# Attention values in four column groups of 32, with denominators from sums of two steps

## The chip, the cores and the metric

The kernel runs on one core of a Trainium2 chip. The metric is the device time of one execution in microseconds (us), the median of several runs. The engines are TensorE (PE, with its weight loads PEld), VectorE (DVE), ScalarE (ACT), GpSimd (POOL) and SyncE (SP, which issues the DMAs here).

## The reference

One "macaron" layer over 2048 tokens of width 512: half a feed-forward block, attention, half a feed-forward block, each on a layer-normalised input and added to the residual. Only attention matters here:

```python
x = x + 0.5 * ffn(layernorm(x))
x = x + attn(layernorm(x))
x = x + 0.5 * ffn(layernorm(x))

# attn: 16 heads of 32 columns, 2048 tokens, causal
q, k, v = heads(x @ w_qkv.T + b_qkv)
scores = q @ k.T / sqrt(32) + causal        # causal: -inf above the diagonal
out = softmax(scores) @ v                   # 16 x 2048 x 32
return merge(out) @ w_out.T + b_out
```

All is in 32-bit floats.

## The kernel before

**Tiling.** The 16 heads are worked in eight head pairs, p = 0 to 7. For a pair the queries go in four blocks of 512 (g = 0 to 3), the keys in chunks of 128 (c). A block g meets the chunks 0 to 4g + 3: the first 4g lie wholly below the diagonal (a *whole step*), the last four cross it (a *diagonal step*; the four of a block are called a quad here). In a diagonal step the first `off` = 0, 128, 256 or 384 queries of the block are left out. So a head pair has 4 + 8 + 12 + 16 = 40 steps. In block 3 six whole steps come first, then the quad, then six whole steps (`around`); in the other blocks the quad comes last.

**One step** (`attend`, `step`). For both heads of the pair (index a) TensorE writes the scores, transposed, keys on the partitions, into a PSUM tile `ps`: first a bf16 matmul that puts minus the row maximum there (`maxrows`, L1311), then the 32-row score matmul (L1320). ACT takes exp into `pt`, 128 x 2 x 512 in SBUF (L1343). In a diagonal step the 128 x 128 block on the diagonal is first copied by ACT (L1336), masked by POOL (`affine_select`, L1337), then exponentiated by ACT in place (L1345). Two steps later (`pending`) `values` multiplies `pt` with the values: this is L1250. Its stationary operand is 64 columns wide: 32 columns of a head's values and 32 columns of ones, side by side in `vaug`, so that one matmul gives the output and the softmax denominator of a head. Head 0 writes partitions 0 to 63 of `av`, head 1 partitions 64 to 127; the ones stand in the middle of `vaug` and serve both. `av` is one PSUM bank (`ps_acc`, one buffer).

**After a block** ACT copies `av` to `both` (L1259). The two denominator rows go by DMA to DRAM (`flat`), come back as 16 x 64 (`packs`), DVE takes the reciprocal (L1277) four steps later, and DMAs bring them back (`back`) and spread them to 32 partitions each (`den`, L1282). From eight steps after the copy on, POOL multiplies a quarter of the block per step, one instruction per head (`chunk`, L1289), into `attnT`. For the last head pair (`direct`) the denominators go by one DMA per head to the partitions of the values (L1266), and DVE takes reciprocals of 128 x 128 (L1286).

**Beside it.** While pair p attends, the row maxima of pair p + 1 are made (`maxima`): score matmuls `pm` (L1185) on TensorE, a mask add on the diagonal (L1199) and a maximum (L1200) on DVE, in as many steps, in the same order, so that the diagonal steps of both fall together. The minus maxima are split into three bf16 parts by POOL (L1211, L1214), transposed by TensorE (L1224) and copied by ACT (L1225). All `ps`, `pm` and projection tiles share seven PSUM buffers (`ps_one`). Pairs 0, 2 and 4 carry projections of queries, keys and values for later pairs, pairs 3, 5 and 7 the output projection (`project_out`, L1135), as filling work after their diagonal steps; pairs 1 and 6 carry none. The last pair has no maxima beside it and takes two steps at a time.

**Order.** The program is scheduled by hand: each engine and each queue runs its instructions in the order in which the code issues them. Per step this is: the score matmuls of both kinds; DVE's maxima; ACT's exp; then the values of two steps before; then what falls due in `after_step`.

Of the kernel before, what the change touches and what calls it, by code (L numbers as in the profile page):

```python
# [10 lines left out]
F32 = mybir.dt.float32  # L11
# [5 lines left out]
ALU = mybir.AluOpType  # L17
AX = mybir.AxisListType

P = 128  # L20
# [3 lines left out]
HD = 32  # L24
NT = S // P
# [10 lines left out]
def macaron_kernel(ctx: ExitStack, tc: tile.TileContext, x, packed, scales, wqk, bqk, wv, bv, wo, bo, out):  # L36
# [1004 lines left out]
    def attention(xT, xT_f, wqk_wv, next_w):  # L1041
        with tc.tile_pool(name="aw", bufs=1) as aw, tc.tile_pool(name="qk", bufs=1) as qkp, tc.tile_pool(
            name="pp", bufs=3
# [30 lines left out]
            dens = [qkp.tile([P, 512], F32, tag=f"den{i}", name=f"den{i}") for i in range(2)]  # L1074
            for t in dens:
                nc.gpsimd.memset(t, 1.0)

            vaug = qkp.tile([P, NT, NPAIR // 2, 3 * HD], F32, tag="vaug", name="vaug")
            for t in range(NT):
                nc.gpsimd.memset(vaug[:, t, :, HD : 2 * HD], 1.0)  # L1080
# [24 lines left out]
            def project_v(half):  # L1105


                def piece(t2):
# [11 lines left out]
                    for i in range(2):  # L1120
                        nc.vector.tensor_tensor(
                            vaug[:, 2 * t2 + i, :, :].rearrange("p h (b d) -> p h b d", d=HD)[:, :, ::2, :],
                            ps[:, i, :].rearrange("p (h b d) -> p h b d", b=2, d=HD),
                            bv_sb[:, bass.ts(half, 256)].rearrange("p (h b d) -> p h b d", b=2, d=HD),
                            ALU.add,
                        )
# [107 lines left out]
            def attend(p, width):  # L1234
# [10 lines left out]
                def values(g, c, off, pt):  # L1245
                    if c == 0:
                        avs[0] = ps_acc.tile([P, 512], F32, tag="acc", name=f"av_{p}_{g}")
                    av = avs[0]
                    for a in range(2):
                        nc.tensor.matmul(  # L1250
                            av[64 * a : 64 * a + 64, off:],
                            lhsT=vaug[:, c, p % 4, HD * a : HD * a + 2 * HD],
                            rhs=pt[:, a, off:],
                            start=(c == 0),
                            stop=(c == order(g)[-1]),
                        )
                    if c == order(g)[-1]:
                        both = an.tile([P, 512], F32, tag="both", name=f"both_{p}_{g}")
                        nc.scalar.copy(both, av)  # L1259
                        rc = dens[g % 2]  # L1260
                        direct = p == NPAIR - 1
                        if direct:

                            for a in range(2):
                                v0, d0 = (0, HD) if a == 0 else (3 * HD, 2 * HD)
                                nc.sync.dma_start(out=rc[v0 : v0 + HD, :], in_=both[d0 : d0 + HD, :])  # L1266
                        else:

                            flat = store.tile([2, 512], F32, tag=f"flat{g % 2}", name=f"flat_{p}_{g}")
                            packs = an.tile([16, 64], F32, tag="packs", name=f"packs_{p}_{g}")  # L1270
                            for a in range(2):
                                d0 = HD + HD * a
                                nc.sync.dma_start(out=flat[a : a + 1, :], in_=both[d0 : d0 + 1, :])
                            nc.sync.dma_start(out=packs, in_=flat.rearrange("a (j n) -> (a j) n", j=8))

                        def inverse():
                            nc.vector.reciprocal(packs, packs)  # L1277
                            back = store.tile([2, 512], F32, tag=f"back{g % 2}", name=f"back_{p}_{g}")
                            nc.sync.dma_start(out=back.rearrange("a (j n) -> (a j) n", j=8), in_=packs)
                            for a in range(2):  # L1280
                                v0 = 3 * HD * a
                                nc.sync.dma_start(out=rc[v0 : v0 + HD, :], in_=back[a].partition_broadcast(HD))  # L1282

                        def chunk(j):
                            if direct:
                                nc.vector.reciprocal(rc[:, bass.ts(j, P)], rc[:, bass.ts(j, P)])  # L1286
                            for a in range(2):
                                v = slice(3 * HD * a, 3 * HD * a + HD)
                                nc.gpsimd.tensor_tensor(  # L1289
                                    dst[quadrant(p, a), bass.ts(4 * g + j, P)],  # L1290
                                    both[v, bass.ts(j, P)], rc[v, bass.ts(j, P)], ALU.mult,
                                )
# [3 lines left out]
                        for j in range(4):  # L1296
                            at((3 if direct else 8) + j, lambda j=j: chunk(j))

                def step(g, c, copied):
# [27 lines left out]
                    def rest():  # L1327
# [18 lines left out]
                        pending.append(lambda args=(g, c, off, pt): values(*args))  # L1346
# [5 lines left out]
                for g in range(NB):  # L1352
                    cs = order(g)
                    for n in range(0, len(cs), width):
                        yield [step(g, c, i > 0) for i, c in enumerate(cs[n : n + width])]
# [234 lines left out]
```

## Time and profile before

| | |
|---|---|
| median of 3 runs | 3216.76 us (3214.57 to 3217.85) |
| profiled execution, time | 3218.9 us |
| its span, first to last instruction | 3217.1 us |
| attention within it | about 1294 to 2104 us |
| busy in 1292 to 2104.3 (812.3 us): PE, DVE, ACT, POOL | 803.0, 487.9, 404.4, 218.0 us |
| mean granted TensorE clock | 0.994 |

The profile's page has these parts: busy time of each engine; the span in slices; DMA queues; the chain of work that ended last, followed back from the last instruction; the costliest groups of instructions by line, with busy time, mean duration in ns and the idle time before them; DMA issues. A timeline lists the instructions of one engine in order: start, duration, engine, line, operation, output and inputs, shape, count, and in brackets the idle time before it with its releaser. A 32-bit matmul appears as two MATMUL records, so "x4" at L1250 is one matmul for each head. Records of matmuls that run side by side overlap, and busy sums count them all; the distance from start to start is the safer reading.

### The profile page before, as it was taken

The numbers are of one execution on the slowest core, as the hardware profiler recorded it, in microseconds if no ns is written. First come the engines' busy times: TensorE is split into PE (matmuls) and PEld (weight loads), VectorE is DVE, ScalarE is ACT, GpSimd is POOL, SyncE is SP. The second block draws the span as 40 slices with busy tenths as digits, with TensorE's granted clock in tenths as the row PEclk, the third lists the DMA queues.
The fourth block names the chain that finished last, engine by engine and source line by source line (L and its number), as shares of the span: only waits on it lengthen the run. The fifth ranks groups of instructions, "written<-read, shape, count | busy, mean of one in ns | idle before, by whom it ended". The sixth has DMA issues, their size and how long they took to land.

```text
span 3217.1 us, 39429 instructions
## 1 busy us (share of the span) xinstructions
PE 3168.7 (98%) x14000; PEld 1978.9 (62%) x14000; DVE 2073.8 (64%) x3011; ACT 1059.2 (33%) x2166; POOL 1300.8 (40%) x1404
## 2 busy tenths in 40 slices
PE   7999999999999999999999999999999999999999
PEld 3556565655656575333334333368888878888887
DVE  7676666666566655566564576487666767766675
ACT  5111111111111131455443456533333343333332
POOL 3757585766767560422121123213222232223222
PEclk9999999999999999999999999999999999999999
DMA  3222221212222200000000000054344445344441
GB/s 137 87 83 109 89 92 62 95 66 89 90 82 107 105 33 7 5 15 7 13 6 6 28 20 8 7 179 140 114 130 131 121 132 164 116 127 128 124 125 59
DMA packets 258851, 260.36 MB, mean 81 GB/s; under 512 B 20392, under 2 KB 221096, under 8 KB 254688
## 3 DMA queue, kind: packets, MB, share of 16 engines
q1 hardware_dynamic: 258656, 257.85, 24.7%
q8 instruction: 111, 1.82, 0.2%
q14 instruction: 84, 0.69, 0.1%
HBM read 176.28 MB, written 79.92 MB: 80 GB/s over the span
## 4 chain that ended last, share of the span: by engine, by line
PE 93%; DVE 2%; ACT 2%; issue 1%; POOL 1%; DMA 0%; SPq 0%; POOLq 0%; DVEq 0%; ACTq 0%
PE d_f L737 12%; PE po L438 12%; PE pu L339 12%; PE pg L339 11%; PE av L1250 8%; PE pod_f L866 7%; PE f_f L737 6%; PE pm L1185 6%; PE pqk L1096 4%; PE pof_f L866 3%; PE e_f L737 3%; PE ps L1311 2%; PE pv L1113 2%; PE poe_f L866 2%; PE pp L1135 2%; PE ps L1320 2%
## 5 line engine op out<-in xcount | busy, mean ns | idle before, releaser
L1200 DVE TENSOR_REDUCE parts<-pm 128x1 f32<-128x512 f32 (+3 forms) x640 | 370.6, 608 | 149.6 <-PE pm L1185 134.1
L1185 PE MATMUL pm<-kT,qT 32*128 32x512 f32 (+3 forms) x1280 | 333.9, 574 | 0.1
L737 PE MATMUL d_f<-ys_f,ring 128*128 128x256 f32 x1216 | 321.4, 385 | 7.1 <-DVE o_f L770 7.0
L1343 ACT ACTIVATE pt<-ps 128x512 f32<-128x512 f32 (+3 forms) x576 | 271.7, 532 | 132.0 <-PE ps L1320 131.3
L1250 PE MATMUL av<-pt,vaug 128*64 128x512 f32 (+3 forms) x1280 | 302.1, 556 | 3.4 <-ACT both L1259 2.6
L1320 PE MATMUL ps<-qT,kT 32*128 32x512 f32 (+3 forms) x1280 | 277.9, 533 | 0.0
L737 PEld LDWEIGHTS d_f<-ys_f,ring 128*128 128x128 f32 x1216 | 228.3, 191 | 54.7 <-DVE o_f L770 21.7
L438 PEld LDWEIGHTS po<-wd,inter 128*128 128x128 f32 x1024 | 194.4, 190 | 77.5 <-issue 56.0
L438 PE MATMUL po<-wd,inter 128*128 128x256 f32 x1024 | 241.1, 379 | 0.0
L791 DVE TENSOR_TENSOR o_f<-o_f,o_f 128x1024 f32<-128x1024 f32 x128 | 203.6, 1601 | 57.5 <-ACT o_f L776 53.7
L339 PE MATMUL pg<-xT_f,w 128*128 128x512 f32 x512 | 240.1, 597 | 0.2 <-ACT u L378 0.2
L339 PE MATMUL pu<-xT_f,w 128*128 128x512 f32 x512 | 238.0, 592 | 0.0
L1337 POOL TENSOR_SCALAR_AFFINE_SELECT pt<-pt 128x256 f32<-128x256 f32 x128 | 52.3, 408 | 396.6 <-ACT pt L1336 388.2
L452 POOL TENSOR_TENSOR xq<-xq,d 128x512 f32<-128x512 f32 x124 | 161.6, 1314 | 92.2 <-DVE xq L446 55.9
L1250 PEld LDWEIGHTS av<-pt,vaug 128*64 128x64 f32 x1280 | 65.5, 135 | 205.0 <-issue 147.1
L791 POOL TENSOR_TENSOR o_f<-o_f,o_f 128x1024 f32<-128x1024 f32 x48 | 128.7, 2682 | 142.7 <-ACT o_f L776 141.5
L881 POOL TENSOR_TENSOR xq<-xq,d_f 128x512 f32<-128x512 f32 x48 | 64.8, 1350 | 293.5 <-DVE xq L875 228.1
L438 PE MATMUL po<-wd,s 128*128 128x256 f32 x768 | 181.4, 379 | 0.0
L438 PEld LDWEIGHTS po<-wd,s 128*128 128x128 f32 x768 | 145.5, 190 | 57.9 <-issue 39.9
L339 PE MATMUL pg<-xsum,w 128*128 128x512 f32 x384 | 177.8, 592 | 0.0
L339 PE MATMUL pu<-xsum,w 128*128 128x512 f32 x384 | 177.7, 592 | 0.0
L881 POOL TENSOR_TENSOR xq_second<-xq_second,d_f 128x512 f32<-128x512 f32 x45 | 61.5, 1366 | 272.9 <-DVE xq_second L875 217.6
(214 smaller groups left out, 6090.9 us busy)
## 6 DMA issues: line engine op xcount, KB each, us to landing
wd_f<-kept SPq DMA_DIRECT2D x112, 256.0 KB
kept<-wd SPq DMA_DIRECT2D x8, 1792.0 KB
xq<-in_x SPq DMA_DIRECT2D x16, 256.0 KB
pk<-in_gate_codes SPq DMA_DIRECT2D x16, 256.0 KB
sc<-in_gate_scales SPq DMA_DIRECT2D x32, 128.0 KB
pk<-in_up_codes SPq DMA_DIRECT2D x16, 256.0 KB
sc<-in_up_scales SPq DMA_DIRECT2D x32, 128.0 KB
pk<-in_down_codes SPq DMA_DIRECT2D x16, 256.0 KB
```

The source lines that it names most:

```text
L339: nc.tensor.matmul(ps, lhsT=a[:, j, :], rhs=b[:, j, :], start=(j == 0), stop=(j == 1))
L438: nc.tensor.matmul(ps[:, j, :], lhsT=a[i][:, k, bass.ts(2 * q + j, P)], rhs=b[i][:, k, :], start=(k == 0), stop=(k == 1),)
L452: adder.tensor_tensor(dst, dst, other, ALU.add)
L737: nc.tensor.matmul(ps[:, k, :], lhsT=fa[k][y], rhs=fb[k][y], start=first and k == 0, stop=True, skip_group_check=True,)
L791: sums.append(lambda: eng.tensor_tensor(dst, dst, other, ALU.add))
L866: nc.tensor.matmul(ps[:, j, :], lhsT=a[:, k, bass.ts(2 * q + j, P)], rhs=wd[:, PLACE[i], k, :], start=new and j == k == 0, stop=True, skip ...
L1096: nc.tensor.matmul(ps, lhsT=w[:, j, k, :], rhs=xT[tb][:, k, :], start=(k == 0), stop=(k == 3))
L1185: nc.tensor.matmul(ps[a][:, :n], lhsT=q[r, bass.ts(4 * g + i, P)], rhs=k[r, kb * 512 : kb * 512 + n], start=True, stop=not on_pe,)
L1200: nc.vector.tensor_reduce(parts[:, a, i, kb : kb + 1], ps[a][:, :n], AX.X, ALU.max)
L1250: nc.tensor.matmul(av[64 * a : 64 * a + 64, off:], lhsT=vaug[:, c, p % 4, HD * a : HD * a + 2 * HD], rhs=pt[:, a, off:], start=(c == 0), s ...
L1320: nc.tensor.matmul(ps[a][:, off:], lhsT=k[r, bass.ts(c, P)], rhs=q[r, g * 512 + off : (g + 1) * 512], start=False, stop=True,)
L1343: nc.scalar.activation(pt[:, a, plain:], ps[a][:, plain:], AF.Exp, scale=scale)
```

## The change

The values operand `vals` no longer holds ones: 32 columns per head. The block's queries are taken as two interleaved halves, h = 0 for the 128-query chunks 0 and 2, h = 1 for the chunks 1 and 3. `columns` issues four matmuls of 32 output columns, one for each head and half, each into its own 32 partitions of `av` (partition group 2a + h) and 256 columns wide; `av` is now 128 x 2 x 256, product 0 the values and product 1 the denominators. The denominators come from separate matmuls with a stationary operand of ones (`ones_f`), once per two steps: the `pt` of two successive steps are added first, and the sum is multiplied. The addition runs on POOL, one instruction per head, for pairs of steps that start at offset 0 both; on DVE, one instruction for both heads with a copy of the columns that only one of the steps has, for the diagonal pairs, and for all pairs of steps of the last head pair. The last two steps of a head pair are not added, and get two sets of denominator matmuls. A sum made in step n is used by the matmuls of step n + 3 (n + 2 at a block's end). `pt` gets four buffers for three, the sums two. Values and denominators of a query now lie on the same partitions, so the last pair needs no DMA for them, and its reciprocals take two chunks at once; the other pairs send four rows of 256 out and back for two of 512.

```diff
-            name="pp", bufs=3
+            name="pp", bufs=4
...
-            dens = [qkp.tile([P, 512], F32, tag=f"den{i}", name=f"den{i}") for i in range(2)]
-            for t in dens:
-                nc.gpsimd.memset(t, 1.0)
-
-            vaug = qkp.tile([P, NT, NPAIR // 2, 3 * HD], F32, tag="vaug", name="vaug")
-            for t in range(NT):
-                nc.gpsimd.memset(vaug[:, t, :, HD : 2 * HD], 1.0)
+            dens = [qkp.tile([P, 256], F32, tag=f"den{i}", name=f"den{i}") for i in range(2)]
+
+            vals = qkp.tile([P, NT, NPAIR // 2, 2 * HD], F32, tag="vals", name="vals")
+            ones_f = aw.tile([P, HD], F32, tag="ones_f", name="ones_f")
+            nc.gpsimd.memset(ones_f, 1.0)
...
-                            vaug[:, 2 * t2 + i, :, :].rearrange("p h (b d) -> p h b d", d=HD)[:, :, ::2, :],
-                            ps[:, i, :].rearrange("p (h b d) -> p h b d", b=2, d=HD),
-                            bv_sb[:, bass.ts(half, 256)].rearrange("p (h b d) -> p h b d", b=2, d=HD),
-                            ALU.add,
+                            vals[:, 2 * t2 + i, :, :].rearrange("p h d -> p (h d)"), ps[:, i, :],
+                            bv_sb[:, bass.ts(half, 256)], ALU.add,
...
-                def values(g, c, off, pt):
-                    if c == 0:
-                        avs[0] = ps_acc.tile([P, 512], F32, tag="acc", name=f"av_{p}_{g}")
-                    av = avs[0]
+                def columns(product, operand, off, **kw):
                     for a in range(2):
-                        nc.tensor.matmul(
-                            av[64 * a : 64 * a + 64, off:],
-                            lhsT=vaug[:, c, p % 4, HD * a : HD * a + 2 * HD],
-                            rhs=pt[:, a, off:],
-                            start=(c == 0),
-                            stop=(c == order(g)[-1]),
-                        )
-                    if c == order(g)[-1]:
-                        both = an.tile([P, 512], F32, tag="both", name=f"both_{p}_{g}")
-                        nc.scalar.copy(both, av)
+                        for h in range(2):
+                            group = slice(HD * (2 * a + h), HD * (2 * a + h) + HD)
+                            if off <= h * P:
+                                dst_ = avs[0][group, product, :].rearrange("p (x n) -> p x n", x=2)
+                                rhs = operand[:, a, :].rearrange("p (x y n) -> p x y n", x=2, y=2)[:, :, h, :]
+                            elif off <= (2 + h) * P:
+                                dst_ = avs[0][group, product, P:]
+                                rhs = operand[:, a, (2 + h) * P : (3 + h) * P]
+                            else:
+                                continue
+                            lhsT = ones_f if product else kw["v"][:, HD * a : HD * a + HD]
+                            nc.tensor.matmul(
+                                dst_, lhsT=lhsT, rhs=rhs, start=kw.get("start", False), stop=True, skip_group_check=True
+                            )
+                two, summed = [], []
+
+                def denominators():
+                    for operand, off in summed.pop(0):
+                        columns(1, operand, off)
+
+                def values(g, n, off, pt):
+                    c = order(g)[n]
+                    if n == 0:
+                        avs[0] = ps_acc.tile([P, 2, 256], F32, tag="acc", name=f"av_{p}_{g}")
+                    columns(0, pt, off, v=vals[:, c, p % 4, :], start=(n == 0))
+                    last = n + 1 == len(order(g))
+                    if (n > 0 and n % 2 == 0) or last:
+                        denominators()
+                    if last:
+                        both = an.tile([P, 2, 256], F32, tag="both", name=f"both_{p}_{g}")
+                        nc.scalar.copy(both, avs[0])
...
-                            for a in range(2):
-                                d0 = HD + HD * a
-                                nc.sync.dma_start(out=flat[a : a + 1, :], in_=both[d0 : d0 + 1, :])
+                            for r in range(4):
+                                nc.sync.dma_start(out=flat[r : r + 1, :], in_=both[HD * r : HD * r + 1, 1, :])
...
+                            for r in range(4):
+                                nc.sync.dma_start(out=rc[HD * r : HD * r + HD, :], in_=back[r].partition_broadcast(HD))
+
+                        def chunk(j):
+                            n = slice(j // 2 * P, j // 2 * P + P)
+                            if direct and j % 2 == 0:
+                                nc.vector.reciprocal(rc[:, n], both[:, 1, n])
                             for a in range(2):
+                                r = slice(HD * (2 * a + j % 2), HD * (2 * a + j % 2) + HD)
                                 nc.gpsimd.tensor_tensor(
+                                    dst[quadrant(p, a), bass.ts(4 * g + j, P)], both[r, 0, n], rc[r, n], ALU.mult
                                 )
...
-                            at((3 if direct else 8) + j, lambda j=j: chunk(j))
+                            at((2 if direct else 8) + j, lambda j=j: chunk(j))
...
-                        pending.append(lambda args=(g, c, off, pt): values(*args))
+                        two.append((pt, off))
+                        if n % 2 == 1:
+                            (one, off_1), (other, off_2) = two
+                            two.clear()
+                            if g + 1 == NB and n + 1 == len(order(g)):
+                                summed.append([(one, off_1), (other, off_2)])
+                            else:
+                                s = pp.tile([P, 2, 512], F32, tag="sum", name=f"sum_{p}_{g}_{n}", bufs=2)
+                                eng = nc.vector if p + 1 == NPAIR or off_2 else nc.gpsimd
+                                if off_1 < off_2:
+                                    eng.tensor_copy(s[:, :, off_1:off_2], one[:, :, off_1:off_2])
+                                for a in range(1 if eng is nc.vector else 2):
+                                    heads = slice(0, 2) if eng is nc.vector else a
+                                    eng.tensor_tensor(
+                                        s[:, heads, off_2:], one[:, heads, off_2:], other[:, heads, off_2:], ALU.add
+                                    )
+                                summed.append([(s, off_1)])
+                        pending.append(lambda args=(g, n, off, pt): values(*args))
```

More of the change, by code (lines that the diff above doesn't have):

```diff
@@ L1260, in values @@
                         rc = dens[g % 2]
                         direct = p == NPAIR - 1
-                        if direct:
-                            for a in range(2):
[L1265 to L1269, printed above, removed]
+                        if not direct:
+                            flat = store.tile([4, 256], F32, tag=f"flat{g % 2}", name=f"flat_{p}_{g}")
@@ L1270, in values @@
                             packs = an.tile([16, 64], F32, tag="packs", name=f"packs_{p}_{g}")
-                            for a in range(2):
-                                d0 = HD + HD * a
-                                nc.sync.dma_start(out=flat[a : a + 1, :], in_=both[d0 : d0 + 1, :])
-                            nc.sync.dma_start(out=packs, in_=flat.rearrange("a (j n) -> (a j) n", j=8))
+                            for r in range(4):
+                                nc.sync.dma_start(out=flat[r : r + 1, :], in_=both[HD * r : HD * r + 1, 1, :])
@@ L1276, in inverse @@
+                            nc.sync.dma_start(out=packs, in_=flat.rearrange("a (j n) -> (a j) n", j=4))
                         def inverse():
                             nc.vector.reciprocal(packs, packs)
-                            back = store.tile([2, 512], F32, tag=f"back{g % 2}", name=f"back_{p}_{g}")
-                            nc.sync.dma_start(out=back.rearrange("a (j n) -> (a j) n", j=8), in_=packs)
-                            for a in range(2):
-                                v0 = 3 * HD * a
-                                nc.sync.dma_start(out=rc[v0 : v0 + HD, :], in_=back[a].partition_broadcast(HD))
@@ L1284, in chunk @@
[L1284 to L1288, printed above, removed]
+                            back = store.tile([4, 256], F32, tag=f"back{g % 2}", name=f"back_{p}_{g}")
+                            nc.sync.dma_start(out=back.rearrange("a (j n) -> (a j) n", j=4), in_=packs)
@@ L1289, in chunk @@
                                 nc.gpsimd.tensor_tensor(
-                                    dst[quadrant(p, a), bass.ts(4 * g + j, P)],
-                                    both[v, bass.ts(j, P)], rc[v, bass.ts(j, P)], ALU.mult,
+                                    dst[quadrant(p, a), bass.ts(4 * g + j, P)], both[r, 0, n], rc[r, n], ALU.mult
                                 )
@@ L1296, in values, with step @@
                         for j in range(4):
-                            at((3 if direct else 8) + j, lambda j=j: chunk(j))
-                def step(g, c, copied):
+                            at((2 if direct else 8) + j, lambda j=j: chunk(j))
+                def step(g, n, copied):
+                    c = order(g)[n]
                     off = max(0, c - 4 * g) * P
@@ L1352, in attend @@
                 for g in range(NB):
-                    cs = order(g)
-                    for n in range(0, len(cs), width):
-                        yield [step(g, c, i > 0) for i, c in enumerate(cs[n : n + width])]
+                    for n in range(0, len(order(g)), width):
+                        yield [step(g, n + i, i > 0) for i in range(width)]
             now = 0
```

## The prediction

> **What bounds the kernel now.** First the page: busy shares (part 1), the chain that ended last (part 4) and the costliest groups (part 5).
>
> ```profile
> PE 3168.7 (98%) x14000; PEld 1978.9 (62%) x14000; DVE 2073.8 (64%) x3011; ACT 1059.2 (33%) x2166; POOL 1300.8 (40%) x1404
> ...
> PE 93%; DVE 2%; ACT 2%; issue 1%; POOL 1%; DMA 0%; SPq 0%; POOLq 0%; DVEq 0%; ACTq 0%
> ...
> L1250 PE MATMUL av<-pt,vaug 128*64 128x512 f32 (+3 forms) x1280 | 302.1, 556 | 3.4 <-ACT both L1259 2.6
> ```
>
> TensorE carries 93% of the chain. The edited matmuls, L1250, take 8% of it (part 4's second line) and hardly wait. Their 302.1 us sums overlapping records, so the true cost comes from the timeline of TensorE in pair 1:
>
> ```profile
> 1438.59 1.08 PE L1250 MATMUL av<-pt,vaug 128*64 128x512 f32 x4
> 1439.60 0.38 PE L1311 MATMUL ps<-wo_bo,ones_b 3*128 3x512 bf16 x1
> ...
> 1450.01 0.65 PE L1250 MATMUL av<-pt,vaug 128*64 128x256 f32 x4
> 1450.59 0.38 PE L1311 MATMUL ps<-wo_bo,ones_b 3*128 3x512 bf16 x1
> ```
>
> Start to next start: 1.01 us for 512 queries, 0.58 for 256; elsewhere in pair 1, 0.80 for 384 and 0.27 for 128 (up to 0.38 in pair 0). So a group costs about 0.15 us to enter and 0.43 per 256 columns. In pair 7, where two steps stand together, 512 + 512 take 1.87: work that follows in the same shape pays 0.86 per 512, with no entry.
>
> Then the stretches of attention: pair 1, pair 3, pair 7.
>
> ```profile
> 1390.00:1475.00 85.00, 83.64 (x607) 27.59 (x604) 59.62 (x124) 50.88 (x132) 25.65 (x70) 1.00 0.03 8
> 1586.00:1686.00 100.00, 100.00 (x636) 32.14 (x636) 69.52 (x140) 50.78 (x132) 24.85 (x68) 1.00 0.02 7
> 2001.50:2104.30 102.80, 96.21 (x515) 35.49 (x514) 50.56 (x80) 51.37 (x135) 28.45 (x65) 0.95 0.04 11
> ```
>
> The columns are length, then busy PE, PEld, DVE, ACT, POOL. The mean share hides the four diagonal steps of each query block. DVE's timeline in pair 1:
>
> ```profile
> 1442.95 0.30 DVE L1199 TENSOR_TENSOR pm<-pm,mask_f 128x128 f32<-128x128 f32 x1 [0.91 <-PE pm L1185]
> ...
> 1449.37 0.18 DVE L1206 TENSOR_REDUCE nmax<-parts 128x8 f32<-128x24 f32 x1
> ```
>
> Between these lines DVE has no idle note: 6.4 us of masks and maxima (1.9, 1.7, 1.45, 1.15 us by step). The scores they read stand in seven PSUM buffers, four used per step, so TensorE may lead DVE by hardly two steps. On a whole step DVE works 1.29 of 2.20 us.
>
> **What the Trainium skill says.** "TensorE: Matmul & The Clock Gate", Part 3 (measured speedup): column groups run side by side; three of 32 columns gave 2.38 times. The trace agrees for two groups of 64 columns (1.01 us for both, beside 0.86 per group of bare streaming); four groups it doesn't show. "TensorEngine Tiling (Array Packing)", Available Configurations and Key Properties: 128x32 is a legal shape of four tiles, and changing shape drains the engine; the 0.15 us entry fits that. "SBUF — State Buffer", Who interferes with whom: a VectorE instruction with two SBUF inputs contends with a GpSimd one that reads SBUF. The trace agrees: the add L791 of 1024 takes 1601 ns, while the like add L621 takes 1226 where GpSimd is idle.
>
> **The change part by part.** *Values.* Four groups of 256 columns run where two of 512 did. Entry and streaming as in the 256 row, 0.58, plus two more group starts 0.01 us apart: 0.60 for 1.01. Bounds: 0.58, or 1.01 if only two groups run at once. Offset 128 still has a 256-column group, 0.60 for 0.80; offsets 256 and 384 have 128 columns, 0.30 each for 0.58 and 0.27.
>
> *Denominators.* Once per two steps, the ones against the sum, in the same shape: 0.43 (half of 0.86), or 0.22 for the second diagonal pair. The last pair of a head pair has no sum and pays twice.
>
> Whole pair of steps: 2.02 − (1.20 + 0.43) = 0.39 saved. Diagonal quad: 2.66 − (1.80 + 0.65) = 0.21. Per head pair: 11 × 0.39 − 0.04 + 4 × 0.21 = 5.1; seven of them 35.6. Pair 7 by its own rows (1.87 becomes 0.60 + 3 × 0.43 less one 0.43, that is 1.46): about 5.5, of which I count 4, since ACT paces parts of it. At its end DVE does two 0.9 us reciprocals for four before TensorE's one 2.33 us wait on GpSimd: 1.7. **TensorE's gain: 41 us.**
>
> *Sums on POOL.* Seven head pairs × 11 whole pairs × two adds of 128x512. The row L1447, same shape, in attention: 1271 ns. So 77 × 2.54 = 196 us on an engine busy 218 of 812: hidden on average. By deadline: exp of step n ends 1.24 us after its scores, the sum 2.54 later, 3.8; TensorE asks after three steps and its values, about 6.4. The four division steps put two multiplies (0.97 us) on the same queue; 2.6 us of slack holds that. Not hidden: the add that ends before a diagonal quad. The quad's first mask on POOL (L1337) queues behind it for some 1.4 us, ACT's own exp behind the mask, and the first DVE sum behind that exp.
>
> *Sums on DVE.* Per quad a copy and an add of 768, a copy and an add of 256. Adds by L621 (1226 for 1024): 0.92 and 0.32. The copy of 256 isn't shown; "VectorE: DVE Perf Modes" (tier table) gives fp32 copies twice an add's rate, so 0.2 to 0.35; I take 0.3. 1.2 + 0.6 = 1.8 us per quad. Behind the waiting sum stand the next maxima, and behind their PSUM buffers TensorE.
> The price, with no filling work (pairs 1 and 6), counted from the end of the first diagonal scores. The scores of the steps take 1.19, 0.93, 0.66 and 0.44 us (TensorE's timeline). TensorE would end step 1's scores at 0.60 + 0.43 + 0.93 = 1.96, step 2's at + 0.60 + 0.66 = 3.22, step 3's at + 0.60 + 0.43 + 0.44 = 4.69, and start the next block at 5.29; that start needs the buffer of step 2's maxima. DVE: step 0 done at 1.9, step 1 at 3.65, the sum at 4.85, step 2 at 6.3. Stall 1.0. In blocks 1 to 3 POOL's add ends at 2.0 (3.8 less the 1.79 us of a step), mask and exp at 2.85, then ACT's copies, exp and masked exp of step 1 at 4.4: DVE starts its sum there, 0.75 later, and the stall is 1.75. Two pairs: 2 × (1.0 + 3 × 1.75) = 12.5. Pairs 3 and 5 add four output projections per quad (0.53 on PE, 0.62 to 0.69 on DVE, a fifth buffer per step, so that step 3 already waits for step 2's first maximum, 8.1 against 7.1, and the next block for step 3's): 1.4 by the same walk, 8 × 1.4 = 11. Pairs 0, 2, 4 have 3.6 us or more of input projections per quad, which cover DVE: 12 × 0.25 = 3. **Stalls: 26 us**; from 0 (the slack of the whole steps takes it) to 2.6 per quad, 73.
>
> *Moved at nothing.* The SP queue gets 4 + 4 row transfers for 2 + 2 per block (0.24 and 0.34 us of issue each): 1.2 us on a chain with eight steps (14 us or more) between copy and product. Pair 7 loses two transfers per block. ACT's copy of 128x512 stays; the 18 memsets (3.4 us) lay on idle POOL; the value bias add keeps its size. If the steps' cover went, a late row would hold POOL's multiplies, then its masks. Four `pt` buffers for three pay for the sum's longer hold; short of that ACT would wait.
>
> Sum: 3218.9 (profiled; 2.1 above the median of 3216.8) − 41 + 26 = 3203.9, so **3202** as a median.
>
> **The rivals.** *A, no stall:* the second and third of DVE's lost us fall where TensorE waits anyway. For: DVE idles 0.9 us per whole step. Against: only two steps of buffers. 3176 to 3190.
> *B, DVE becomes the bound in every quad:* its sums wait for ACT and for POOL's lock, maxima wait behind them, TensorE behind the buffers. Decides from 41/28 = 1.5 us per quad. For: DVE has no idle in the quad. Against: three of seven pairs have filling work. At 2.6 us per quad (1.75 and two POOL multiplies' 0.45 each): +32, 3249.
> *C, the change doesn't do what it says:* four groups run two at a time. Then per head pair the values stay and 11 × 0.86 + 1.72 + 4 × 1.29 = 16.3 us of denominators come on top, eight times 131: 3348. For: no row shows four streams of 128 rows. Against: four row groups overlap at L1185 and L1320 (1.19 us for a bf16 and a fp32 pass of 512 in each).
>
> **How the numbers follow.** About 0.2%, 6.4 us, is what a measurement here can tell from none. Forecast (stalls of 20 to 34 us, 3195 to 3210) 0.40; A 0.20; stalls that nearly cancel the gain 0.13; B beyond that 0.19; C 0.08. Faster 0.60, same 0.13, slower 0.27. The range is 3175 to 3242, which leaves out C and B's upper end.
>
> **What would show it.** Right: values of a whole step at 0.60 us and denominators 0.43 later in TensorE's timeline; steps of 1.79 and 2.22 by turns; idle or stretched score matmuls (L1185, L1311) released by DVE at the end of quads in pairs 1, 3, 5, 6, none in 0, 2, 4. Wrong: 1.0 us per value group (C); DVE-released idle after every quad (B); no such idle (A); denominators that wait for POOL's sum in the whole steps, which I priced at nothing.

## The result, and the profile after

The changed kernel takes **3240.05 us** (3231.5 to 3242.44, four runs) against 3216.88 us for the kernel before: a ratio of 1.0068 [1.0049, 1.0087], slower. The forecast was 3202 and faster. The profiled execution took 3239.97 us, with a span of 3238.2 us and a mean granted clock of 0.987 (0.994 before). Outside attention the two kernels agree within some 2 us; the loss lies in attention.

First the page of the changed kernel, the same three lines as in the prediction and, third here, that of the score matmuls of the maxima:

```profile
PE 3168.0 (98%) x16496; PEld 2022.4 (62%) x16496; DVE 2130.8 (66%) x3142; ACT 1063.9 (33%) x2166; POOL 1501.5 (46%) x1541
...
PE 90%; DVE 5%; POOL 1%; ACT 1%; issue 1%; DMA 1%; SPq 0%; POOLq 0%; DVEq 0%; ACTq 0%
...
L1181 PE MATMUL pm<-kT,qT 32*128 32x512 f32 (+3 forms) x1280 | 376.3, 593 | 16.4 <-DVE parts L1196 15.0
...
L1256 PE MATMUL av<-pt,vals 128*32 128x256 f32 (+1 forms) x2432 | 194.2, 376 | 0.3 <-ACT both L1278 0.2
```

TensorE's share of the chain fell from 93% to 90% and DVE's rose from 2% to 5%. The score matmuls of the maxima (L1185 before, L1181 now) had 0.1 us of idle time ahead of them; now they have 16.4, ended by DVE. Their mean also rose, from 574 to 593 ns, with nothing changed about them. Their row before:

```profile
L1185 PE MATMUL pm<-kT,qT 32*128 32x512 f32 (+3 forms) x1280 | 333.9, 574 | 0.1
```

The edited matmuls themselves do what the diff says. TensorE's timeline in pair 1, two whole steps:

```profile
1442.41 0.64 PE L1256 MATMUL av<-pt,vals 128*32 128x256 f32 x8
1442.98 0.39 PE L1324 MATMUL ps<-wo_bo,ones_b 3*128 3x512 bf16 x1
...
1444.16 0.64 PE L1256 MATMUL av<-pt,vals 128*32 128x256 f32 x8
1444.62 0.62 PE L1256 MATMUL av<-sum,ones_f 128*32 128x256 f32 x8
1445.17 0.38 PE L1324 MATMUL ps<-wo_bo,ones_b 3*128 3x512 bf16 x1
```

Start to next start: 0.57 us for the values (1442.41 to 1442.98), and 1.01 for values and denominators (1444.16 to 1445.17). Two steps cost 1.58 us where they cost 2.02. A step takes 2.19 and 1.75 us by turns (1442.98, 1445.17, and the next at 1446.92).

Then the stretches. Pairs 1, 3 and 7, from each pair's first score matmul to the next pair's, columns as before:

```profile
1404.00:1493.20 89.20, 84.06 (x892) 33.15 (x888) 63.26 (x137) 49.54 (x129) 54.43 (x90) 0.94 0.03 8
1606.30:1709.50 103.20, 100.89 (x956) 40.71 (x952) 75.07 (x157) 50.65 (x130) 53.94 (x95) 1.00 0.03 7
2027.00:2125.60 98.60, 90.14 (x860) 39.39 (x857) 64.34 (x100) 51.65 (x136) 35.50 (x65) 0.97 0.02 8
```

Pair 1 is idle on TensorE for 5.1 us and its clock is 0.94, where it was 1.00 before. Cut at the same marks, all the pairs compare so (us; in parentheses the time at half the TensorE clock, read from the record of the granted clock):

| kernel | pair 0 | 1 | 2 | 3 | 4 | 5 | 6 | 7 | sum |
|---|---|---|---|---|---|---|---|---|---|
| before | 107.4 | 81.4 | 109.2 | 103.5 | 130.4 | 96.4 | 80.8 | 102.8 (10.2) | 811.8 |
| after | 109.6 (3.4) | 89.2 (10.2) | 113.1 (10.2) | 103.2 | 124.6 | 102.3 (13.7) | 90.6 (13.7) | 98.6 (6.8) | 831.2 |

Pairs 4 and 7 gain and pair 3 stays as it was (0.3 us less); pairs 0, 1, 2, 5 and 6 lose, and these five are the ones that have half clock where the kernel before had none. DVE's timeline shows what happens at the end of a quad (pair 1, block 0):

```profile
1412.02 0.29 DVE L1196 TENSOR_REDUCE parts<-pm 128x1 f32<-128x128 f32 x1
1412.35 0.16 DVE L1202 TENSOR_REDUCE nmax<-parts 128x8 f32<-128x8 f32 x1
1412.43 0.28 DVE L1370 COPY sum<-pt 128x256 f32<-128x256 f32 x1
1414.74 0.42 DVE L1373 TENSOR_TENSOR sum<-pt,pt 128x256 f32<-128x256 f32 x1 [2.03 <-ACT pt L1358]
1415.09 1.28 DVE L1196 TENSOR_REDUCE parts<-pm 128x1 f32<-128x512 f32 x2
```

The second diagonal sum stands idle for 2.03 us, waiting for ACT's exp, and the maxima of the next block (1415.09) stand behind it. Why the exp is so late is read from POOL's and ACT's timelines of the same moment:

```profile
1412.57 0.22 POOL L1207 CAST split<-nmax 128x8 bf16<-128x8 f32 x1 [2.25 <-DVE nmax L1202]
...
1413.71 0.22 POOL L1207 CAST split<-left 128x8 bf16<-128x8 f32 x1
1413.86 0.41 POOL L1350 TENSOR_SCALAR_AFFINE_SELECT pt<-pt 128x256 f32<-128x256 f32 x1
...
1414.29 0.42 ACT L1358 ACTIVATE pt<-pt 128x256 f32<-128x256 f32 x1 [2.65 <-POOL pt L1350]
```

It is a **loop through three engines**. DVE makes the block's last maxima and `nmax`; POOL splits `nmax` in five instructions (1.3 us, 1412.57 to the mask's start), and only then does the mask of the fourth diagonal step come up in its queue; ACT's exp waits for the mask; DVE's sum waits for the exp. So the sum can't start until some 2.4 us after `nmax`, however fast DVE was. This holds where the fourth diagonal step is also the step that makes `nmax`: in blocks 0 to 2 of pairs 0 to 6, 21 blocks, each with 2.0 to 2.4 us of idle time before the sum. In block 3 the quad stands between whole steps, and `nmax` comes six steps after it. There the same sum waits 0 to 0.3 us; in pair 1:

```profile
1482.30 0.28 DVE L1370 COPY sum<-pt 128x256 f32<-128x256 f32 x1
1482.73 0.45 DVE L1373 TENSOR_TENSOR sum<-pt,pt 128x256 f32<-128x256 f32 x1
1483.10 1.27 DVE L1196 TENSOR_REDUCE parts<-pm 128x1 f32<-128x512 f32 x2
```

So the changed kernel holds a comparison of its own: the same two instructions, with the split ahead of the mask and without it. DVE's row for the sum, by form, in attention:

```profile
L1373 DVE TENSOR_TENSOR sum<-pt,pt 128x256 f32<-128x256 f32 x32 | 14.8, 464 | 48.7 <-ACT pt L1358 48.4
```

48.4 us of waiting for 14.8 of work, some 44 of them in the 21 blocks (seven of the 32 are the blocks 3, four are pair 7's). TensorE meets it one step later: its matmuls for the maxima need the PSUM buffers that DVE hasn't read, and then it runs at half speed:

```profile
1414.04 1.12 PE L1181 MATMUL pm<-kT,qT 32*128 32x512 f32 x2
1415.82 0.37 PE L1324 MATMUL ps<-wo_bo,ones_b 3*128 3x512 bf16 x1 [0.67 <-DVE parts L1196]
1416.42 1.01 PE L1181 MATMUL pm<-kT,qT 32*128 32x512 f32 x1 [0.23 <-DVE parts L1196]
...
1422.06 1.08 PE L1256 MATMUL av<-pt,vals 128*32 128x256 f32 x8
```

The windows of the same stretch, with the granted clock in the third column from the right:

```profile
1413.30:1416.70 3.40, 2.50 (x23) 0.82 (x14) 1.96 (x4) 1.97 (x4) 0.82 (x4) 0.99 0.03 7
1416.70:1423.50 6.80, 6.80 (x46) 2.39 (x47) 2.64 (x5) 3.21 (x6) 2.48 (x2) 0.50 0.07 21
```

After 0.9 us of idle time in 3.4, TensorE runs 6.8 us at half clock: the values at 1422.06 take 1.08 us where they took 0.64. All ten stretches of half clock in pairs 0 to 6 begin within 3.3 us of such a sum in a block 0, 1 or 2; none follows a block 3.

### The profile page after: what moved, and what is told of

Same layout as the page of the kernel before. It is cut to its first block, busy times and chain, and to the rows that moved or that the text cites. A ratio compares the mean times of both kernels' runs of the same rounds, so it can differ in the third digit from the quotient of the medians.

```text
span 3238.2 us, 44948 instructions
## 1 busy us (share of the span) xinstructions
PE 3168.0 (98%) x16496; PEld 2022.4 (62%) x16496; DVE 2130.8 (66%) x3142; ACT 1063.9 (33%) x2166; POOL 1501.5 (46%) x1541
## 4 chain that ended last, share of the span: by engine, by line
PE 90%; DVE 5%; POOL 1%; ACT 1%; issue 1%; DMA 1%; SPq 0%; POOLq 0%; DVEq 0%; ACTq 0%
PE d_f L737 12%; PE po L438 12%; PE pg L339 12%; PE pu L339 12%; PE pod_f L866 7%; PE pm L1181 7%; PE f_f L737 6%; PE av L1256 5%; PE pqk L1094 4%; PE pof_f L866 3%; PE e_f L737 3%; PE ps L1324 2%; PE pv L1111 2%; PE poe_f L866 2%; DVE parts L1196 2%
## 5 line engine op out<-in xcount | busy, mean ns | idle before, releaser
L1181 PE MATMUL pm<-kT,qT 32*128 32x512 f32 (+3 forms) x1280 | 376.3, 593 | 16.4 <-DVE parts L1196 15.0
L1333 PE MATMUL ps<-qT,kT 32*128 32x512 f32 (+3 forms) x1280 | 294.3, 563 | 0.0
L1373 POOL TENSOR_TENSOR sum<-pt,pt 128x512 f32<-128x512 f32 x154 | 192.2, 1270 | 132.7 <-ACT pt L1356 113.3
L438 PEld LDWEIGHTS po<-wd,inter 128*128 128x128 f32 x1024 | 194.8, 190 | 77.2 <-issue 55.4
L339 PE MATMUL pg<-xT_f,w 128*128 128x512 f32 x512 | 240.6, 598 | 0.0
L339 PE MATMUL pu<-xT_f,w 128*128 128x512 f32 x512 | 238.0, 592 | 0.0
L1256 PE MATMUL av<-pt,vals 128*32 128x256 f32 (+1 forms) x2432 | 194.2, 376 | 0.3 <-ACT both L1278 0.2
L1256 PEld LDWEIGHTS av<-pt,vals 128*32 128x32 f32 x2432 | 53.1, 110 | 203.4 <-issue 171.1
L393 POOL TENSOR_TENSOR u<-u,u 128x512 f32<-128x512 f32 x64 | 81.7, 1277 | 211.4 <-ACT u L390 211.4
L339 PE MATMUL pg<-xsum,w 128*128 128x512 f32 x384 | 179.6, 597 | 0.0
```

The source lines that it names most:

```text
L339: nc.tensor.matmul(ps, lhsT=a[:, j, :], rhs=b[:, j, :], start=(j == 0), stop=(j == 1))
L438: nc.tensor.matmul(ps[:, j, :], lhsT=a[i][:, k, bass.ts(2 * q + j, P)], rhs=b[i][:, k, :], start=(k == 0), stop=(k == 1),)
L1181: nc.tensor.matmul(ps[a][:, :n], lhsT=q[r, bass.ts(4 * g + i, P)], rhs=k[r, kb * 512 : kb * 512 + n], start=True, stop=not on_pe,)
L1256: nc.tensor.matmul(dst_, lhsT=lhsT, rhs=rhs, start=kw.get("start", False), stop=True, skip_group_check=True)
L1333: nc.tensor.matmul(ps[a][:, off:], lhsT=k[r, bass.ts(c, P)], rhs=q[r, g * 512 + off : (g + 1) * 512], start=False, stop=True,)
L1373: eng.tensor_tensor(s[:, heads, off_2:], one[:, heads, off_2:], other[:, heads, off_2:], ALU.add)
```

## The experiments

The theory to test, called W in the expectations: the loss is the loop just shown, and half the clock follows from it. Its rivals: DVE simply has **too much work** in the quads (near to the prediction's rival B), or **POOL's long sums** of whole steps are in the way (both are K in the expectations), or the **32-column matmuls** lower the clock by themselves (H). That half the clock is a loss by itself, and not only a sign of the stall, is a theory apart, which the expectation of f calls C (it has nothing to do with the prediction's rival C). The results of a, b, d and e lie outside the ranges expected under W, each on the side away from the rivals: the loop costs more than was put down for it (d), and the matmuls gain more (c).

**What the matmuls alone gain: c_no_sums.** The sums are left out; the denominators multiply a constant tile of ones, with the same matmuls, so the output is not that of the attention.

```diff
-                                s = pp.tile([P, 2, 512], F32, tag="sum", name=f"sum_{p}_{g}_{n}", bufs=2)
...
-                                summed.append([(s, off_1)])
+                                summed.append([(fixed, off_1)])
```

> The additions are left out: the denominator matmuls multiply a constant tile of ones, so the denominators are not those of the softmax. TensorE's matmuls are the same in number, size and order as in the changed kernel; neither POOL nor DVE has a sum to make. This is TensorE's side of the change alone. Theory W and rival K: the 41 us that were forecast for TensorE come out, 3172 to 3182, and the clock is as before the change (0.994). Rival H: the clock stays near 0.987 and the time over 3195.

3164.34 us, ratio 0.9836 [0.9821, 0.985]. Attention takes 758.1 us, 53.7 less than before: 40.3 in pairs 0 to 6 and 13.4 in pair 7. So the gain is there, larger than expected, and all that is lost hangs on the sums. There is no half clock anywhere in attention, with every 32-column matmul in place: H is out.

**Only the second sum later: a_second_sum_late.** The second diagonal sum of a block is issued on DVE after the next step's maxima. The same instructions run, for the same columns; `add` holds the copy and the addition, and the last two lines open the next step's `rest`.

```diff
+                                if off_2 == 3 * P and p + 1 < NPAIR:
+                                    held.append(add)
+                                else:
+                                    add()
...
+                        while held:
+                            held.pop(0)()
```

> The second diagonal sum of each block (copy and add of 256 columns on DVE) is issued one step later, behind the next step's maxima; all else as in the changed kernel, the matmuls of TensorE in the same order. Theory W (the wait): in the changed kernel this sum holds DVE idle for 48 us in all (28 blocks at 1.7 us), because it needs an exp that waits for a POOL mask that waits for POOL's split of the maxima that DVE has just made; that wait stalls TensorE and drops its clock. Then most of the loss goes: 3190 to 3210 us, few half-clock windows in pairs 1, 2, 5, 6. Rival K (DVE's added work of 1.6 us per block and POOL's late masks stall TensorE, the wait itself lies under cover): no more than 10 us better than the changed kernel, 3230 to 3240. Rival H (the 32-column matmuls themselves [...]lower the clock): clock and time as in the changed kernel.

3186.57 us, ratio 0.9906 [0.9891, 0.9921]: moving it is worth 53 us and turns the loss into a gain. Its waits in attention, under the same query as those of the changed kernel; first the changed kernel, then this one (us in total, times, longest):

```profile
DVE sum L1373 <- ACT pt L1358: 52.2, 32, 2.4
PEld pm L1181 <- DVE parts L1196: 41.9, 29, 2.8
```

```profile
DVE sum L1376 <- ACT pt L1360: 12.5, 20, 1.0
PEld pm L1181 <- DVE parts L1196: 10.0, 23, 1.0
```

The sum's wait falls from 52.2 to 12.5 us, and that of TensorE's weight loads for the maxima from 41.9 to 10.0. Its pairs 1 and 2:

```profile
1399.40:1479.50 80.10, 77.99 (x895) 31.68 (x891) 64.03 (x138) 49.23 (x129) 54.35 (x90) 1.00 0.04 9
1479.50:1583.30 103.80, 103.76 (x957) 41.39 (x954) 67.28 (x141) 52.49 (x133) 52.58 (x90) 1.00 0.04 12
```

DVE does as much work in pair 1 as in the changed kernel (64.03 us for 63.26), POOL as much (54.35 for 54.43), and the pair is 9.1 us shorter, the clock whole. That speaks against DVE's and POOL's work as the cause of the loss.

**The quads without sums: b_quads_apart.** The diagonal steps get two sets of denominator matmuls instead of a sum on DVE; POOL keeps its sums.

```diff
-                            if g + 1 == NB and n + 1 == len(order(g)):
+                            if (g + 1 == NB and n + 1 == len(order(g))) or (off_2 and p + 1 < NPAIR):
```

> No diagonal pair of steps is summed in head pairs 0 to 6: both steps get denominator matmuls of their own (0.43 + 0.22 us more of TensorE per block, 18 us in all), DVE has neither work nor wait for them. POOL's sums of the whole steps stay. Theory W: the loss of the changed kernel goes here too, with 18 us of TensorE paid: 3200 to 3215. Rival K with DVE's work as the cause: about the same, and 10 to 20 us better than with the late second sum. Rival K with POOL's late masks as the cause, and rival H: 3245 to 3258.

3189.45 us, ratio 0.9912 [0.9895, 0.9929]. It pays 28 × (0.43 + 0.22) = 18 us of TensorE and ends beside a. In pairs 0 to 6 it is 13.8 us longer than c, less than those 18: POOL's 154 sums of whole steps cost nothing that can be seen. As the cause of the loss POOL's long sums fall: here they all run, and the kernel is faster than before.

**The wait alone, in the kernel before: d_before_with_wait.** No sum, no new matmul; DVE copies one column of the fourth diagonal exp once per block.

```diff
                             nc.scalar.activation(own, own, AF.Exp, scale=scale)
+                            if off == 3 * P and p + 1 < NPAIR:
+                                nc.vector.tensor_copy(glance, own[:, 0, 0:1])
```

> The kernel before, and in it one DVE copy of a single column per block (head pairs 0 to 6) that reads the masked exp of the fourth diagonal step, issued where the changed kernel issues its second diagonal sum. It brings the wait with next to no work (28 copies of some 0.1 us). Theory W: DVE idles 45 to 60 us more there, and the kernel before becomes slower by 12 to 35 us, 3229 to 3252. Rival K and rival H: within 5 us of the kernel before.

3257.71 us, ratio 1.0125 [1.0109, 1.014]. A copy of one column, 28 times, costs 41 us; in 21 of the 28, the blocks 0 to 2, it waits 2.2 us or more, in the blocks 3 less than 0.5. Its wait, from the waits in attention:

```profile
DVE glance L1348 <- ACT pt L1346: 50.7, 28, 2.5
```

Pairs 0 to 6 have 44.3 us of half clock, where the kernel before has none. No sum is needed for such a loss: the wait is enough.

**The loop cut at POOL: e_mask_first.** The sums stay where the change put them. POOL's split of `nmax`, the same five instructions, is put into a function `parts_of` that is called after the step's mask and exp (`rest`) instead of ahead of them.

```diff
+                            tail.append(parts_of)
...
                     for _, _, rest, _ in steps:
                         rest()
+                    while tail:
+                        tail.pop(0)()
```

> The changed kernel with one move on POOL's queue: the split of the minus maxima (five instructions, 1.4 us) is issued behind the mask of the same step and not ahead of it. DVE's second sum stays where the change put it. Theory W with this link (DVE makes the maxima, POOL splits them, only then masks; ACT's exp and DVE's sum wait for the mask): the wait of the second sum falls from 1.7 to 0.3 us per block, and the time to that of the late second sum, 3183 to 3197. Rival W2 (the sum waits for ACT or for the scores, not for POOL's split): the wait stays over 1 us per block, 3225 to 3240.

3178.63 us, ratio 0.9881 [0.9866, 0.9896]. ACT's wait for masks in the changed kernel, and then the same wait and the sum's wait for ACT in this one:

```profile
ACT pt L1358 <- POOL pt L1350: 101.7, 91, 3.6
```

```profile
ACT pt L1362 <- POOL pt L1354: 55.9, 91, 3.6
DVE sum L1377 <- ACT pt L1362: 8.5, 12, 1.0
```

The sum's wait was 52.2 us in the changed kernel. A change of order on POOL, with DVE's order untouched, is worth 61 us. That fits the loop and nothing that lies on DVE alone.

**The wait again, with the loop cut: j_before_wait_mask_first.** Kernel d with the edit of e.

> The kernel before with the glance of d (DVE copies one column of the fourth diagonal exp at each block's end), and with POOL's split of the row maxima put behind the mask. If the price of the glance is the loop (maxima, split, mask, exp, DVE), the 50.7 us that DVE waited there fall below 15, TensorE's half clock in attention (44.4 us in d) to about the 10.2 of before, and the time back to 3213 to 3222. If any instruction of DVE that reads a fresh exp costs TensorE time, whatever POOL does first, it stays near 3257.

3216.47 us, ratio 0.9997 [0.9989, 1.0006]: the 41 us are gone. The glance's row:

```profile
DVE glance L1352 <- ACT pt L1350: 3.6, 12, 0.5
```

The same copy that cost 41 us has no cost that shows once its operand doesn't pass through a queue that waits for DVE. (The edit with no copy at all was not run: what it gains by itself, if anything, is in this result.) Half clock is back to the 10.2 us of pair 7.

**What half the clock costs: f_clock_held.** The changed kernel, with twelve bf16 matmuls of 128 columns, whose result is overwritten, at the fourth diagonal step of each block and the two steps after it, in pairs 1, 2, 5 and 6.

```diff
+                        if a == 0 and p in (1, 2, 5, 6) and whole_n in (3, 4, 5, 11, 12, 13, 23, 24, 25, 33, 34, 35):
+                            for _ in range(12):
+                                nc.tensor.matmul(ps[a][:, 384:], lhsT=ones_b, rhs=identb, start=True, stop=True)
```

> The changed kernel, and in head pairs 1, 2, 5 and 6 twelve more bf16 matmuls of 128x128 by 128 columns (about 0.7 us) at the head of the fourth diagonal step and of the two steps after it, into the score tile that is then written over. They fill idle time of TensorE and shorten no wait. Theory C (the half-clock windows follow from idle time and cost on their own): half-clock time in these pairs falls from 47.8 us to under 20, and although up to 32 us of matmuls are added, the time stays within 12 us of the changed kernel or falls below it, 3220 to 3250. Rival C0 (the clock costs nothing beyond the stall): the windows may go, the time rises by 15 us or more, 3255 to 3270.

3230.99 us, ratio 1.0045 [1.003, 1.006]. Pairs 1 and 2:

```profile
1405.50:1491.70 86.20, 86.12 (x1039) 38.98 (x1035) 63.35 (x138) 49.50 (x129) 54.50 (x90) 1.00 0.03 9
1491.70:1604.50 112.80, 112.80 (x1103) 49.00 (x1099) 66.87 (x142) 52.98 (x133) 52.76 (x90) 1.00 0.04 11
```

TensorE has no gap left and its clock is whole, and these pairs are 3.0 and 0.3 us *shorter* although matmuls were added; the four pairs together 10.8. (These are lengths of one execution each; the whole times of the two kernels, 3229.86 to 3237.01 here and 3231.5 to 3242.44 there, overlap.) DVE's wait is what it was (52.5 us by the same row). So half the clock is a loss of its own. Its size can be estimated from two pairs that this kernel leaves alone (one execution each): pair 3 had 6.8 us of half clock here and none in the changed kernel, and took 106.4 for 103.2; pair 0 had 3.4 us more and took 111.2 for 109.6. Both give 0.47 us lost per us of half clock, and TensorE's idle time in these two pairs is the same in both kernels within 0.1 us (2.4 and 2.3, 4.4 and 4.4). The changed kernel's own executions fit: the one of 3231.5 us had a mean clock of 0.990, those of 3240 had 0.987; that is some 19 us less of half clock and 8.5 us less time. The changed kernel has 51.2 us of half clock in pairs 0 to 6 (the sum of its row in the table), so the estimate is 24 us.

**Both diagonal sums late: h_both_late.** As a, with the first diagonal sum held back too.

```diff
-                                if off_2 == 3 * P and p + 1 < NPAIR:
+                                if off_2 and p + 1 < NPAIR:
```

> Both diagonal sums of a block are issued one step later. With the second late the first still waits for ACT (some 0.6 us in most blocks). If that wait is what is left of the stall in pairs 1 and 6 (the late mask behind POOL's sum of the whole steps, as forecast), 3180 to 3184. If what is left is DVE's added work, within 2 us of the late second sum, 3184 to 3189.

3198.4 us, ratio 0.994 [0.9925, 0.9955]: a miss, 12 us worse than a. The excess is in pairs 0 (111.0 for 104.3) and 2 (108.1 for 103.8), and ACT waits 115.4 us for masks, 101.6 in a. A late first sum stands ahead of the maxima that end the block, so that `nmax`, and with it the mask behind the split, may come later; that is argued, and which step of these pairs pays for it stays open.

**A better version: g_best and i_mask_first_apart.** g is a with the quads apart in pairs 1 and 6; i is e with the same.

> The second diagonal sum late as in the first experiment, and in head pairs 1 and 6, which have no filling work, no sums in the diagonal quads (denominators of both steps apart). Pairs 1 and 6 took 80.0 and 80.5 us with the late sum and 77.2 and 77.2 with the quads apart; so 6 us under the late second sum: 3181 (3178 to 3184). If pair lengths don't add up this way, 3185 to 3188.

> The changed kernel with POOL's split of the row maxima put behind the mask, and in pairs 1 and 6 without the sums of the diagonal steps (two sets of denominator matmuls for them, 0.43 + 0.22 us of TensorE more per quad, 5.2 us in eight quads). If DVE's sums still hold TensorE up in the pairs without filling work (those pairs took 79.0 and 78.7 us with the mask first, 77.2 in both kernels with the quads apart), these two pairs fall to 77.2 and the time is 3175. If only the wait in the loop had a price, the 5.2 us of matmuls come on top: 3184.

g: 3180.4 us, ratio 0.9884 [0.9867, 0.99], as expected. i: 3177.31 us, ratio 0.9877 [0.986, 0.9893]. In i, pairs 1 and 6 took 77.2 and 77.3 us, as expected if the sums' work still holds these two pairs, where e took 79.0 and 78.7; on the whole time e and i can't be told apart. What held e's pairs is in its timeline of pair 1, at the first diagonal sum of block 1:

```profile
1415.80 0.52 POOL L1306 TENSOR_TENSOR attnT<-both,den 32x128 f32<-32x128 f32 x1
1415.92 1.22 DVE L1377 TENSOR_TENSOR sum<-pt,pt 128x768 f32<-128x768 f32 x1
1416.40 1.00 POOL L1354 TENSOR_SCALAR_AFFINE_SELECT pt<-pt 128x256 f32<-128x256 f32 x1
...
1417.86 0.37 PE L1181 MATMUL pm<-kT,qT 32*128 32x128 f32 x1 [0.68 <-DVE parts L1196]
```

This is the stall that the prediction walked through: the sum delays the maxima, and TensorE waits for a buffer. The instructions of DVE and POOL also stretch each other, the later one each time: the add began 0.12 us after a POOL multiply and took 1.22 us, the mask began inside the add and took 1.00. The mask takes 0.41 where it begins with no add running, and the add 0.95 where it begins with POOL idle. The Trainium skill says in "SBUF — State Buffer", Who interferes with whom, that a VectorE instruction with two SBUF inputs contends with a GpSimd one that reads SBUF; the trace agrees.

Both e and i beat the kernel before and the changed one. i gains 1.2% on the one and 62.7 us on the other.

## Why the prediction was wrong

Attention by terms, from the pairs' lengths; the sums close (−40.3 − 4.2 + 12.7 + 51.2 = +19.4):

| term | predicted | measured | from |
|---|---|---|---|
| matmuls, pairs 0 to 6 | −35.6 | −40.3 | c less before |
| pair 7 and its end | −5.7 | −4.2 | after less before |
| sums other than the second one's wait | +26 | +12.7 | a less c, pairs 0 to 6 |
| the second sum's wait | 0 | +51.2 | after less a, pairs 0 to 6 |

**The step that failed** is the one under *Sums on DVE* that prices the second diagonal sum as "a copy and an add of 256", 0.6 us of work, and lets it start when DVE comes to it. The walk asked of the first sum when its exp would be there; of the second it didn't ask. The runs show in its place a start some 2.4 us after `nmax` in 21 blocks, and 51.2 us lost to it where 0 was put. The kernel before would have told. Its timelines at a block's end (POOL, ACT):

```profile
1450.82 0.22 POOL L1211 CAST split<-left 128x8 bf16<-128x8 f32 x1
1450.97 0.41 POOL L1337 TENSOR_SCALAR_AFFINE_SELECT pt<-pt 128x256 f32<-128x256 f32 x1
1451.41 0.42 ACT L1345 ACTIVATE pt<-pt 128x256 f32<-128x256 f32 x1 [2.75 <-POOL pt L1337]
```

The fourth exp ended at 1451.8, 2.5 us after the `nmax` of 1449.37, for the same reason. Then it harmed nobody, since only `values` of two steps later needed it. The change made DVE a reader of it, ahead of the next maxima.

**The second failed step** is what is not in the working: the TensorE clock. The sum took stalls at their own length. Of these 51.2 us, 24 are half clock by f's rate; the rest, some 27, is put to the stall. That is a remainder: TensorE's idle time by its records rose by 15.7 us only (22.3 in pairs 0 to 6, 6.6 in a), and what the other 11 are is open. By the same estimate the changed kernel would have come out near the kernel before without the clock (3240 − 24 = 3216).

**Point by point.**

- *Values and denominators*: right. 0.57 and 0.44 for the 0.60 and 0.43 forecast; a pair of steps saves 0.44 where 0.39 was said, which is most of the 4.7 us by which the term was too small.
- *Pair 7*: the total is near by luck, its parts are not right. Its matmuls and end gain 13.4 us (c), part of that because its 10.2 us of half clock go too, and the sums take back 9.2 (98.6 for 89.4), 6.8 us of half clock among it; the prediction had priced only the matmuls and the reciprocals, and discounted them.
- *POOL's sums*: 1270 ns for 1271, and hidden (b). What the late mask behind a POOL sum costs, 0.75 us per block in the walk, no run shows apart.
- *DVE's first sums*: the copies take 0.28 us for 0.3, the adds 0.95 (1.22 behind POOL) and 0.42 for 0.92 and 0.32. Pairs 1 and 6 cost 8.7 us for 12.5 and pairs 0, 2 and 4 3.9 for 3, near enough; pairs 3 and 5 cost nothing for 11. The walk for these two was wrong: in a their lengths, 97.6 and 90.5, are those without any sums; which of its steps failed is open.
- *SP's DMAs and the other things moved at nothing*: no run here shows a cost.
- *Readings of lines*: two are off and change no sum: the 302.1 us of L1250, like the other busy times, count overlapping records once (1280 of 556 ns would be 712), and 0.86 us is what both column groups of a step take together, not each; that groups run side by side it doesn't show (the last section does).

**The rivals.** C is out: 0.57 us per group. A is out as a forecast of this kernel, but close to a (3186.57), e and i: it is what the change gives without the loop. B named the nearest cause, sums that wait for ACT with the maxima behind them, and 3249 for 3240; but it priced the first sum and POOL's multiplies, in every quad. The wait that cost most is the second sum's, in 21 quads, and about half of its price is the clock; so the near number is luck.

**The signs to look for.** Steps of 1.79 and 2.22 by turns: 1.75 and 2.19. DVE-released idle in pairs 1, 3, 5 and 6 and none in 0, 2 and 4: wrong for 0 and 2, which lost 5.3 and 9.3 us to the wait; only pair 4 lost nothing to it: DVE waits there as long, but TensorE has no idle time. No denominators held by POOL's sum in whole steps: right, as far as b can show.

## What to carry to other kernels

When a queue gets a new reader of some result, trace that result back through every queue that it crosses, and look whether one of them waits for the reader itself: such a loop has a length of its own (here 2.4 us, whatever DVE's average load; only the filling work of pair 4 covered it whole), and it is visible in the trace of before as a wait that harms nobody yet. Price a new stall on TensorE at more than its length, since the clock may follow. Before giving up on a change like this, move the one instruction that waits, or the one it waits behind: here that turned 0.7% slower into 1.2% faster.

## What the runs showed of the hardware

**The TensorE clock falls after short stalls.** The record of the granted clock is made of windows of 3.413 us, at 1.0 or 0.5. In the changed kernel ten stretches of half clock lie in pairs 0 to 6; in the 3.41 us ahead of each, TensorE was idle for 0.68 to 1.11 us by its records (in d's ten, 0.53 to 0.94). The Trainium skill gives the window, in "TensorE: Matmul & The Clock Gate", Part 1 (3413 ns, with half the rate after at least one idle window); the length agrees, but here a window idle for a fifth of its time was enough. Idle time is not the whole condition: other windows with 1.09 and 1.33 us idle weren't followed by half clock.

**A few small matmuls hold it.** The twelve of f, recorded as 0.84 us together, kept the clock whole in all four pairs that had them (47.8 us of half clock to none).

**Four column groups of 32 run side by side in 32-bit floats**: 0.57 us for four of 256 columns over 128 rows, and 0.44 more for four behind them in the same shape. In the kernel before, 32-bit matmuls of all 128 columns over 128 rows (L339 in the first feed-forward block) follow each other at 0.86 us per 512, which is 0.43 for 256; so four groups together take as long as one matmul.
